# Layer 1 of a four-layer image kernel: a ninth VectorE product in third-slot jobs, and B rows spread in mid-unit in first-slot jobs

## The chip, the cores and the metric

The kernel runs on one core of a Trainium2 chip. The metric is the device time of that core in microseconds (us). Five engines work side by side, each with its own queue of instructions that it takes in order: TensorE (PE; its weight loads are listed as PEld), VectorE (DVE), ScalarE (ACT), GpSimd (POOL) and SyncE (SP, which here issues nearly all DMAs). They wait for one another through semaphores.

## The reference

The input is 8 images of 192 channels and 56 x 56 points, in float32. Four layers follow one another, each of the form x = x + f(group_norm(x)): layer 0 is an involution, layers 1 to 3 are Mamba blocks. The change concerns layer 1 alone. Its core is this recurrence (shortened):

```python
xn = layer_norm(x)                       # 192 channels, as three slices of 64
xs = stack of the three slices           # each goes through the same block
xi, z = split(xs @ in_proj_W.T)          # 512 inner channels each
xc = silu(causal_conv4(xi) + conv_b)
dbl = xc @ x_proj_W.T
dt = softplus(dbl[:4] @ dt_proj_W.T + dt_proj_b)
B, C = dbl[4:20], dbl[20:36]             # 16 states
h = h * exp(dt * A) + (dt * xc) * B      # for each point, channel and state
y = sum over states of h * C + xc * D
y = (y * silu(z)) @ out_proj_W.T
```

After it come a skip connection, a second layer norm over the three slices, and a projection to 192 channels. The points of an image form one sequence of 3136 steps, and h runs along it.

## The kernel before

**Tiling.** A chunk is 8 rows of an image, 448 points; there are 7 chunks to an image and 56 in all. In layer 1 each chunk makes three *jobs*, one for each slice of 64 channels; the number of the slice (0, 1, 2) is the job's *slot*, `jobs[i][0]`. So first-slot, second-slot and third-slot jobs follow in turn, 168 in all. A job has 512 inner channels in 4 groups of 128 (`nd == 4`), and each group is scanned in 4 *units* (`q`), so a job has 16 units, numbered `m` = 0 to 15, and layer 1 has 2688, numbered `k`. A unit holds 32 channels times 4 states on 128 partitions, and 4 runs of 448 points in the free dimension.

**What a unit needs.** (1) ScalarE writes exp(dt * A) into PSUM in two halves (`decays`, L761). (2) The product (dt * xc) * B goes into the buffer `uhg`. Either GpSimd makes it, from a B row that a DMA has spread over the partitions (`inputs_by_pool`, L782), or VectorE makes it, from a B row that a TensorE matmul has spread into a PSUM bank (`spread_b`, L749, then `inputs_by_vector`, L789). That bank, `banks.b`, has one buffer: the next spread must wait until the product that reads the present one is done. (3) VectorE scans the two halves in place (`scan`, L793). (4) ScalarE saves the last column for the next chunk (`keep`, L797). (5) GpSimd multiplies in place by the C row (`readout`, L802). (6) TensorE sums over the states into `y` (`reduce`, L811; the first unit of a group begins with L808). (7) One group later VectorE multiplies `y` into the gate (`gated`, L827), which frees the only `y` bank.

**Who makes which product.** `pool_units(i)` (L720 to L724) lists the units of a job whose product GpSimd makes: 1, 3, 7, 9, 11, 13 and 15 in every job, and besides unit 5 in first-slot jobs and in the last job, unit 6 in the others. So GpSimd and VectorE make eight each.

**Order.** The loop at L882 writes the order out by hand. In unit k every engine gets, in this order: the reduce of unit k-3; half 0 of scan k; the decays of unit k+1, half 0; GpSimd's product for unit k+2, if it is GpSimd's; the readout of unit k-2; VectorE's product for unit k+1, if it is VectorE's; the second planned place; half 1 of scan k; `keep`; the decays of k+1, half 1. In a job's unit 3 the product of unit 5, if VectorE's, is made early, right after scan 3 (L934).

Where the spread stands is the second thing of the change. In layers 2 and 3 (`nd == 3`) `spread_b(k + 2)` is called in mid-unit, ahead of the second planned place. In layer 1 (`nd == 4`) `spread_next_b(k + 1)` is called at the unit's end, behind the second planned place and ahead of half 1 of the scan. It spreads the next row that a VectorE product will want, as soon as the product before it has been put into VectorE's queue.

**The plan.** Each unit has two places in which steps of the *next* job are run: its convolution (L1069), the Silu block of ScalarE with its two table loads (L616, L597, L589; unit 3), the x-projection (L621), the delta projections (L632, L633, L655, moved out by L637 and L660), the Softplus block (L663, L589; unit 7 while a first-slot job runs, unit 9 otherwise), L667 and L670 behind it, and the gates (L1087, moved out by L694). The closing layer norm and projection of a chunk run during the first-slot job of the next one; the opening layer norm of the next chunk runs during the second-slot job. `nothing` (L817) adds matmuls with zeros where TensorE has little to do.

## Time and profile before

| | |
|---|---|
| median of 3 runs | 24,679.64 us (24,675.72 to 24,681.13) |
| the profiled execution | 24,712.5 us, span 24,710.4 us, mean granted TensorE clock 0.837 |
| busy over the span | POOL 94%, DVE 92%, PE 83%, ACT 69% |
| layer 1, from its first scan to layer 2's | 1,620.8 to 16,879.6 us |
| one chunk of it (window 13,790.6 to 14,060.3 us), its three jobs | 95.9 + 89.6 + 84.2 us |
| GpSimd busy in that chunk | 269.0 of 269.7 us |
| VectorE busy in that chunk | 252.3 of 269.7 us |
| one GpSimd product, one readout (layer 1, mean) | 3,992 ns, 3,675 ns |
| one VectorE product, one half scan (layer 1, mean) | 1,996 ns, 2,009 ns |
| one spread, full clock | 0.36 us |

A busy share is a mean over the span; what a change in layer 1 is worth shows in a chunk of layer 1. An engine's idle time is put down to what ended it. Durations overlap a little at their ends, so the step from one scan to the next counts for more than the sum of the means: a half scan takes 1.92 us from start to start, a VectorE product 1.93, a GpSimd product 3.95, a readout 3.64.

### The profile page before, as it was taken

To read this page: it belongs to the slowest core of one execution; us is meant where nothing else is said; L and a number is where in the kernel's file an instruction comes from. 1 tells how busy PE (TensorE), PEld (TensorE's weight loads), DVE (VectorE), ACT (ScalarE), POOL (GpSimd) and SP (SyncE) were. 2 spreads that over 40 slices of the span, in tenths; PEclk is the share of its full clock that TensorE was granted. 3 is DMA by queue.
4 is the path that set the end of the run, shared out by engine and by line. 5 is a ranking of instruction groups with operands and counts; after the bars stand their busy time and mean duration, and the time that the engine had idled before them with its cause. 6 is when DMAs were issued, how large, how long until landed. Compare 5 with 4: busy or idle time off the path is not lost.

```text
span 24710.4 us, 238275 instructions
## 1 busy us (share of the span) xinstructions
PE 20615.4 (83%) x74330; PEld 6482.2 (26%) x74330; DVE 22834.6 (92%) x15771; ACT 17044.6 (69%) x32578; POOL 23167.0 (94%) x6886
## 2 busy tenths in 40 slices
PE   8988888888888888888888888887888888888888
PEld 2222222222222222222222222222333322333332
DVE  8989999999999999999999999997999998999999
ACT  2247777777777777777777777776777776777776
POOL 5679999999999999999999999997999987999999
PEclk9987777778777887887887788788899888999998
DMA  4433333333333333333333333333444443444443
GB/s 109 109 107 128 128 127 128 126 124 129 127 126 128 128 128 123 129 128 126 128 128 126 126 129 128 127 127 114 135 135 140 140 137 122 140 144 141 140 140 128
DMA packets 1209092, 3171.54 MB, mean 128 GB/s; under 512 B 166444, under 2 KB 470596, under 8 KB 1207688
## 3 DMA queue, kind: packets, MB, share of 16 engines
q1 hardware_dynamic: 1205016, 3155.25, 38.8%
q8 instruction: 583, 9.55, 0.2%
q14 instruction: 693, 5.68, 0.1%
q10 hardware_dynamic: 2800, 1.06, 0.0%
HBM read 2438.45 MB, written 555.55 MB: 121 GB/s over the span
## 4 chain that ended last, share of the span: by engine, by line
DVE 28%; PE 22%; POOL 19%; issue 12%; ACT 12%; DMA 5%; SPq 1%; DVEq 0%; POOLq 0%; ACTq 0%
DVE uhg L793 19%; POOL uhg L802 12%; POOL uhg L782 6%; DVE uhg L789 6%; ACT da L761 5%; DMA rows<-bc 4%; PE y L811 4%; PE mm L655 3%; PE mm L1152 2%; PE mm L429 1%; PE mm L632 1%; PE y L808 1%; PE y_inv L467 1%; DVE prod L441 1%; PE mm L1099 1%
## 5 line engine op out<-in xcount | busy, mean ns | idle before, releaser
L793 DVE TENSOR_TENSOR_SCAN uhg<-da,uhg 128x898 f32<-128x898 f32 x8064 | 15893.3, 2010 | 729.2 <-ACT da L761 716.0
L802 POOL TENSOR_TENSOR uhg<-uhg,rows 128x1792 f32<-128x1792 f32 x4032 | 14734.2, 3676 | 185.3 <-ACT carry L797 181.6
L761 ACT ACTIVATE da<-rep,k 128x448 f32<-128x448 f32 x16128 | 10261.3, 636 | 1762.8 <-DVE uhg L793 1437.1
L782 POOL TENSOR_TENSOR uhg<-rep,rows 128x1792 f32<-128x1792 f32 x1906 | 7610.6, 3993 | 738.3 <-DMA rows<-bc 500.3
L811 PE MATMUL y<-uhg,k 128*32 128x448 f32 x32256 | 4647.7, 654 | 696.6 <-POOL uhg L802 692.4
L789 DVE TENSOR_TENSOR uhg<-rep,b 128x1792 f32<-128x1792 f32 x2126 | 4246.9, 1998 | 296.8 <-PE b L749 252.4
L797 ACT COPY carry<-uhg 128x4 f32<-128x4 f32 x4032 | 786.1, 195 | 3420.0 <-DVE uhg L793 3351.9
L817 PE MATMUL y<-w_d,k 128*128 128x448 f32 (+1 forms) x5276 | 2380.7, 553 | 0.0
L808 PE MATMUL y<-xc,w_d 128*128 128x448 f32 x2016 | 1526.7, 853 | 1004.1 <-DVE zs L827 1003.8
L811 PEld LDWEIGHTS y<-uhg,k 128*32 128x32 f32 x32256 | 680.2, 116 | 3492.2 <-issue 1917.4
L1125 PE MATMUL mm<-v,w_in 96*128 96x448 f32 x2688 | 1335.2, 625 | 188.3 <-ACT zs L696 85.0
L817 PEld LDWEIGHTS y<-w_d,k 128*128 128x128 f32 x5276 | 988.2, 203 | 1567.0 <-issue 1541.5
L1087 PE MATMUL mm<-xs,k 64*128 64x448 f32 x1344 | 893.1, 769 | 509.6 <-ACT zs L694 479.2
L655 PE MATMUL mm<-dbl,w_dt 36*128 36x448 f32 (+1 forms) x2016 | 1290.4, 756 | 1.9 <-ACT k L637 0.5
L749 PE MATMUL b<-k,k 96*128 96x448 bf16 x2126 | 809.0, 381 | 460.3 <-DVE uhg L789 459.8
L1069 PE MATMUL mm<-xs,k 128*128 128x448 f32 x2688 | 1119.8, 558 | 18.6 <-DMA xs<-xg 8.1
L667 PE MATMUL mm<-xc,k 128*128 128x448 f32 x2016 | 1032.6, 630 | 94.4 <-DVE dt L670 94.4
L1152 PE MATMUL mm<-xin,w_conv 128*128 128x448 f32 x2688 | 1077.9, 543 | 0.9 <-ACT xin L696 0.9
L441 DVE TENSOR_TENSOR prod<-mm,shifted 128x448 f32<-128x448 f32 x1680 | 929.9, 613 | 152.8 <-PE mm L429 77.1
L632 PE MATMUL mm<-dbl,k 16*16 16x448 f32 x1120 | 696.7, 711 | 441.7 <-ACT dbl L625 434.1
L808 PEld LDWEIGHTS y<-xc,w_d 128*128 128x128 f32 x2016 | 467.7, 269 | 1836.0 <-DVE zs L827 1348.9
L670 DVE TENSOR_TENSOR dt<-dt,mm 128x448 f32<-128x448 f32 x1008 | 594.0, 611 | 329.3 <-ACT dt L663 134.4
(138 smaller groups left out, 19659.1 us busy)
## 6 DMA issues: line engine op xcount, KB each, us to landing
rep<-ops SPq DMA_DIRECT2D x4032, 448.0 KB, 5.8
ops<-dt SPq DMA_DIRECT2D x1008, 448.0 KB, 3.1
rows<-bc SPq DMA_DIRECT2D x1960, 224.0 KB, 6.2
shifted<-xpad SPq DMA_DIRECT2D x672, 179.0 KB, 4.4
xg<-stream SPq DMA_DIRECT2D x168, 336.0 KB, 3.8
xr<-stream SPq DMA_DIRECT2D x168, 336.0 KB, 4.9
stream<-xr SPq DMA_DIRECT2D x112, 336.0 KB, 7.3
xs<-xg SPq DMA_DIRECT2D x224, 112.0 KB, 2.3
```

Of the source, the lines that this page charges most:

```text
L441: nc.vector.tensor_mul(prod.rearrange("p (h w) -> p h w", w=WW), fbs[item][: 128 if kind == "four" else CP, :T].rearrange("p (h w) -> p h ...
L655: nc.tensor.matmul(u.dps[j][:, :T], lhsT=w.dtw[:, j * 128 : (j + 1) * 128], rhs=u.dbl[:nk, :], start=True, stop=True)
L761: nc.scalar.activation(t[:, 64 + 449 * r : 512 + 449 * r], reps[k // NQ][:, 2 * h + r, 0, :], AF.Exp, scale=w.neg_a[:, j * NR + 2 * h + r, ...
L782: nc.gpsimd.tensor_mul(uhg[k][:, :, 1:], reps[k // NQ][:, :, 1, :], b)
L789: nc.vector.tensor_mul(uhg[k][:, :, 1:], reps[k // NQ][:, :, 1, :], b)
L793: nc.vector.tensor_tensor_scan(v, banks.da[h][:, 63:961], v, 0.0, ALU.mult, ALU.add)
L802: nc.gpsimd.tensor_mul(v, v, us[i].rows[1, q].unsqueeze(1).to_broadcast([128, NR, T]))
L808: nc.tensor.matmul(ys[k // NQ][:, :T], lhsT=w.dd[:, j, :], rhs=us[i].xc[:, j, :], start=True, stop=False)
L811: nc.tensor.matmul(y[32 * r : 32 * r + 32, :T], lhsT=fold, rhs=uhg[k][:, r, 1:], start=False, stop=(q == NQ - 1))
L817: nc.tensor.matmul(ys[k // NQ][:, : nd * 112], lhsT=zeros, rhs=w.dd.rearrange("p j e -> p (j e)")[:, : nd * 112], start=False, stop=False,)
L1125: nc.tensor.matmul(pm[:, :T], lhsT=w.inw[:, k, m * 128 : (m + 1) * 128], rhs=ck.v[:, k, :], start=(k == 0), stop=(k == NCT - 1),)
L1152: nc.tensor.matmul(pm[:, :T], lhsT=w.convd[:, j, k, :], rhs=ck.xin[:, j, k : k + T], start=(k == 0), stop=(k == 3))
```

## The change

In third-slot jobs unit 6 leaves GpSimd's list: GpSimd makes seven products there and VectorE nine (0, 2, 4, 5, 6, 8, 10, 12, 14). The last job of the layer stays as it was. The row for it is spread by TensorE, one spread more in each of 55 jobs. In first-slot jobs the rows are spread as in layers 2 and 3: `spread_b(k + 2)` in mid-unit k, where before the same row was spread at the end of unit k-1. In second-slot and third-slot jobs `spread_next_b` stays at the unit's end.

```diff
         def pool_units(i):
 
             if nd == 4:
-                return {1, 3, 6 if jobs[i][0] and i + 1 < len(jobs) else 5, 7, 9, 11, 13, 15}
+                fixed = {1, 3, 7, 9, 11, 13, 15}
+                if jobs[i][0] == 0 or i + 1 == len(jobs):
+                    return fixed | {5}
+                return fixed | ({6} if jobs[i][0] == 1 else set())
             return {1, 3, 7, 9, 11} | ({6} if i + 1 == len(jobs) else set())
...
+            rows_between = nd == 3 or jobs[i][0] == 0
...
                 inputs_by_vector(k + 1)
-            if nd == 3 and k + 2 < n_units:
+            if rows_between and k + 2 < n_units:
                 spread_b(k + 2)
             bg.run(plan[2 * m + 1])
-            if nd == 4:
+            if not rows_between:
                 spread_next_b(k + 1)
```

## The prediction

> **What bounds the kernel now.** First the page, part 2 (busy tenths in 40 slices of 618 us; layer 1 fills slices 3 to 27):

> ```profile
> DVE  8989999999999999999999999997999998999999
> POOL 5679999999999999999999999997999987999999
> PEclk9987777778777887887887788788899888999998
> ```

> Both VectorE and GpSimd stand at 9 in layer 1, so shares don't tell which one binds. Next, one steady chunk by its three jobs (columns: window; its length; busy us and instructions of PE, PEld, DVE, ACT, POOL; granted clock; DMA share; GB/s):

> ```profile
> 13790.60:13886.50 95.90, 82.26 (x239) 23.10 (x241) 87.09 (x55) 66.54 (x126) 95.90 (x27) 0.73 0.36 121
> 13886.50:13976.10 89.60, 71.58 (x240) 21.28 (x235) 83.63 (x51) 67.10 (x129) 89.37 (x24) 0.80 0.35 119
> 13976.10:14060.30 84.20, 70.67 (x248) 20.64 (x248) 81.62 (x49) 62.24 (x120) 83.77 (x23) 0.87 0.41 143
> ```

> GpSimd works 269.0 of 269.7 us, VectorE 252.3. Then the waits in that chunk, first GpSimd's, then VectorE's (total, times, longest):

> ```profile
> POOL uhg L782 <- DMA rows<-bc: 0.4, 1, 0.4
> POOL uhg L802 <- ACT carry L797: 0.2, 1, 0.2
> ```

> ```profile
> DVE uhg L793 <- ACT da L761: 6.5, 7, 1.6
> DVE uhg L789 <- PE b L749: 4.4, 2, 3.8
> DVE zs L827 <- PE y L811: 2.5, 2, 1.4
> DVE dt L670 <- PE mm L667: 1.3, 2, 0.9
> ```

> GpSimd sets the pace: 48 readouts of 3.64 and 24 products of 3.95 us, start to start, are 269.5 us, the chunk. VectorE idles 17 us, but only part of that is GpSimd's doing, and this part is all that a lighter GpSimd can give back. Two numbers from the timeline (start of a readout less the end of the `keep` before it) say how close VectorE is: 9.5 us at the end of a third-slot job, where GpSimd is far behind, and 0.1 us at unit 4 of the second-slot job, where it has caught up and hangs on VectorE. So one change of pace of 0.1 us there makes VectorE the bound.

> **The change part by part**, in us per chunk, on the profiled execution (24,712.5, span 24,710.4; it ran 33 over the median).

> *The product leaves GpSimd:* 3.95 less in each of 55 third-slot jobs. GpSimd then needs 265.5.

> *It comes to VectorE:* +1.93, between the halves of scan 5; that job has 81.6 of 84.2 busy, so nothing there hides it. Behind it on VectorE stand scan 5 half 1 and scan 6; `keep` 5 and readout 5 wait for those. Readout 5 had 7.1 us to spare and keeps about 1.2.

> *Its spread* (one weight load, one matmul, 0.36) takes the place at the end of unit 4 that unit 8's row had, about 3.8 us before the product wants it; unit 8's row goes to the end of unit 5, still some 5 us early. In front of reduce 3 this is 0.4, against 1.93 that VectorE is later. Cost 0; were TensorE over 3.8 late, it would show on VectorE one for one. The B row for GpSimd (q = 2) is still loaded and nobody reads it: SP's queue and its DMAs do not change. Zero matmuls do not change either.

> *What GpSimd's relief gives back.* Third-slot job, unit 10:

> ```profile
> 14028.13 2.03 DVE L793 TENSOR_TENSOR_SCAN uhg<-da,uhg 128x898 f32<-128x898 f32 x1 [0.75 <-ACT da L761]
> 14029.09 0.96 PE L811 MATMUL y<-uhg,k 128*32 128x448 f32 x8 [2.09 <-POOL uhg L802]
> 14029.98 1.77 PE L667 MATMUL mm<-xc,k 128*128 128x448 f32 x4
> 14031.04 1.37 DVE L670 TENSOR_TENSOR dt<-dt,mm 128x448 f32<-128x448 f32 x2 [0.88 <-PE mm L667]
> ```

> The reduce waits for a late readout, L667 stands behind it, VectorE waits 0.88. With GpSimd 5.9 (3.95 + 1.93) nearer this goes: -0.88. In the first-slot job, units 6 and 7:

> ```profile
> 13825.64 0.55 PE L749 MATMUL b<-k,k 96*128 96x448 bf16 x1
> 13826.63 1.72 PE L811 MATMUL y<-uhg,k 128*32 128x448 f32 x8 [0.44 <-POOL uhg L802]
> 13828.28 3.35 PE L655 MATMUL mm<-dbl,w_dt 36*128 36x448 f32 x4
> 13828.42 0.62 DVE L827 TENSOR_TENSOR zs<-zs,y 128x448 f32<-128x448 f32 x1 [1.43 <-PE y L811]
> 13831.67 0.63 ACT L660 ACTIVATE dt<-mm,k 128x448 f32<-128x448 f32 x1 [0.86 <-PE mm L655]
> ```

> Readout 3 holds the reduce, this holds VectorE's gate and L655, and L655 holds ScalarE's Softplus block, after which VectorE waits 0.74 + 0.98 + 1.47. What remains without GpSimd shows in the chunk from 4,861.3 us: GpSimd enters it 1.6 us less far behind (7.8 against 9.4), the gate waits are gone, and its first-slot job takes 93.9 instead of 96.0. The waits on ScalarE's blocks stay even there (2.84 at unit 4, 3.19 at units 7 and 8, 0.94 at unit 13). So -2.1 and no more. The changed kernel enters the job about 4.5 behind, past that point.

> *First-slot jobs, the spread in mid-unit.* Unit 8's row (0.55 at half clock, above) goes from in front of reduce 3 to behind L655: the Softplus chain starts up to 0.55 earlier. Between 0 and -0.55 I take -0.5, since ScalarE waits for L655. Two products get their row late, if TensorE keeps its times: unit 6 (behind L621) by 0.86 on average, unit 8 (behind L655) by 1.16. For unit 8, 0, since scan 7's second half waits 0.74 and L670 0.98 anyway. For unit 6, between 0 and 0.86, I take 0: its spread leaves the end of unit 3 (0.4) and TensorE's 0.7 wait for GpSimd at unit 4 goes. The other rows have 2.1 to 6.9 to spare. TensorE no longer waits for VectorE with a spread in unit 9 (3.2); only the layer norm stands behind, for which VectorE does not wait: 0.

> *The seam to the second-slot job.* Unit 2's row was spread at the end of the first-slot job's unit 15. That call is gone, and `spread_next_b` comes next at the end of unit 0, behind eight passes of L1069:

> ```profile
> 13888.87 0.36 PE L749 MATMUL b<-k,k 96*128 96x448 bf16 x1
> 13890.05 3.27 PE L1069 MATMUL mm<-xs,k 128*128 128x448 f32 x8
> 13892.29 2.00 DVE L789 TENSOR_TENSOR uhg<-rep,b 128x1792 f32<-128x1792 f32 x1
> ```

> L1069 ends at 13,893.3, the product started at 13,892.3: +1.1 (over all jobs 1.24 on average, 0.5 to 3.2 in eight of ten). It lies on VectorE just ahead of the place where GpSimd has 0.1 to spare, so nothing covers it.

> Sum for an ordinary chunk: -2.1 - 0.5 + 1.1 + 1.93 - 0.88 = -0.45, and GpSimd idles 3.5. In the 8 chunks that open an image GpSimd already catches up in the first-slot job (104.0 long, readouts 0.1 us behind at its end), so of its 2.6 only 0.5 counts, and the third-slot wait is 1.16: -0.5 + 1.1 + 1.93 - 1.16 = +1.4. Together 47 x -0.45 + 8 x 1.4 = -10. So 24,702 for an execution like the profiled one, **24,670** against the median.

> *TensorE's clock* is the least certain term. In the second-slot job VectorE waits for unit 5's row 3.85 in the steady chunk, where half clock was granted for 6.8 us from unit 3 on, 2.14 in the chunk at 4,861 (3.4 us of half clock) and 0.55 in chunks without it; the mean is 2.95. I leave it as it is. [...]

> **The rivals.**

> *GpSimd stays the bound.* All of its 3.95 comes through: 55 x 3.95 = -217, 24,463. For it: its waits, 0.6 us a chunk. Against: VectorE would have to give up 5.9 us of waits plus the seam's 1.1, and I find 3.5 that are GpSimd's. Half of it needs luck with the clock (3.85 becoming 2.14: 47 x -1.7 = -80, 24,590).

> *VectorE is the bound already.* Nothing is recovered, and the late rows are paid on VectorE: 1.93 + 1.1 + 0.86 = 3.9 a chunk, +214, 24,894. For it: the 0.1 us at unit 4 of the second-slot job. Against: the waits on L811 and L667 above. It decides once less than 2.1 of the 3.5 us comes back.

> *The change does nothing* is ruled out: 55 instructions leave GpSimd's queue and join VectorE's.

> **How the numbers follow.** A measurement here tells about 0.2% (49 us) from no change. My forecast has 0.46; its own range is 24,590 to 24,750 (1.5 us a chunk for the clock): 0.34 within 0.2%, 0.07 below, 0.05 above. The faster rival, in part or in full, has 0.27 (0.01 of it within 0.2%); the slower one 0.27 (0.03 within). So faster 0.33, same 0.38, slower 0.29. From 24,520 to 24,830 leaves out about 0.09 at each end.

> **What would show it.** Right: GpSimd idle 3 to 4 us a chunk, waiting for `carry`; the gate waits of first-slot jobs gone and those jobs near 93.5; a new wait of about 1.1 for `b` in second-slot unit 1; third-slot jobs near 85.2. Wrong, faster: GpSimd still without idle time, chunks near 266. Wrong, slower: chunks over 271, with waits of VectorE for `b` in first-slot units 5 and 7, or the Softplus waits grown under half clock.

## The result, and the profile after

The changed kernel takes 24,794.57 us (median; 24,772.89 to 24,824.98) against 24,681.13 us for the kernel before on the same chip: a ratio of 1.0043, 95% interval 1.0031 to 1.0055. It is slower by 0.43%, 113 us. The forecast was 24,670, so the sign was missed, though the time lies inside the stated range of 24,520 to 24,830.

The page of the changed kernel (its profiled execution took 24,794.57 us, span 24,792.7), parts 2, 4 and 5; lines from 724 to 902 have moved down by 3, later ones by 4:

```profile
DVE  8989999999999999999999999997999998999999
POOL 6679999999999999999999999997999987999999
PEclk9987777777777777777777777778899888999999
...
DVE 35%; PE 27%; ACT 14%; issue 13%; POOL 5%; DMA 5%; SPq 1%; DVEq 0%; POOLq 0%; ACTq 0%
...
L805 POOL TENSOR_TENSOR uhg<-uhg,rows 128x1792 f32<-128x1792 f32 x4032 | 14737.2, 3674 | 479.0 <-ACT carry L800 468.8
...
L670 DVE TENSOR_TENSOR dt<-dt,mm 128x448 f32<-128x448 f32 x1008 | 599.5, 612 | 444.3 <-ACT carry L800 162.5
```

The shares of part 2 hardly move. What moved is who waits for whom. GpSimd's share of the chain that ended last is 5% (it was 19%), and its readouts now wait 479 us, 469 of them for ScalarE's carries. The change did take the pace away from GpSimd. The chain runs over VectorE, TensorE and ScalarE instead. `L670` stands out: a small VectorE operation with 444 us of idle time in front of it.

Layer 1, from its first scan to layer 2's, went from 15,258.8 to 15,375.1 us: the whole loss is there (between these two executions the rest came out 34 us shorter). By jobs (from scan to scan; means of 56 first-slot, 56 second-slot and 55 third-slot jobs, without the last one, which runs into layer 2): first-slot jobs 96.29 to 93.99, second-slot 89.03 to 90.54, third-slot 85.04 to 88.01; -2.30 + 1.51 + 2.97 = +2.2 us a chunk. Three chunks that follow one another, windows by job, as in the fence of the prediction (window; length; busy us and instructions of PE, PEld, DVE, ACT, POOL; granted clock; DMA share; GB/s):

```profile
13584.24:13676.91 92.67, 81.16 (x237) 23.02 (x239) 86.74 (x55) 66.63 (x126) 92.25 (x26) 0.73 0.38 124
13676.91:13765.77 88.86, 69.86 (x240) 20.91 (x236) 83.74 (x51) 67.10 (x129) 87.05 (x24) 0.83 0.35 121
13765.77:13853.79 88.02, 77.09 (x250) 22.07 (x250) 83.62 (x51) 62.53 (x120) 85.81 (x24) 0.80 0.39 136
13853.79:13946.45 92.66, 81.05 (x237) 22.93 (x239) 86.76 (x55) 66.62 (x126) 92.29 (x26) 0.73 0.38 126
13946.45:14038.35 91.90, 73.38 (x240) 21.77 (x236) 83.96 (x52) 67.09 (x129) 87.48 (x24) 0.80 0.35 117
14038.35:14126.61 88.26, 76.02 (x249) 22.19 (x250) 83.62 (x51) 62.47 (x120) 85.51 (x23) 0.82 0.40 137
14126.61:14220.96 94.35, 79.11 (x237) 22.89 (x239) 86.96 (x55) 66.64 (x126) 92.41 (x26) 0.76 0.38 122
14220.96:14312.10 91.14, 72.05 (x240) 21.53 (x236) 83.74 (x52) 67.11 (x129) 86.67 (x24) 0.80 0.34 116
14312.10:14400.01 87.91, 76.92 (x250) 22.11 (x250) 83.62 (x50) 62.46 (x120) 86.14 (x24) 0.80 0.41 140
```

Chunks take 269.6, 272.8 and 273.4 us, in this order, again and again; chunks that open an image are longer. First-slot jobs fell to 92.7, below the forecast of 93.5, in two of the three. Third-slot jobs take 88, not 85.2, in all. Two things in these windows led to the experiments. VectorE's waits over the three chunks:

```profile
DVE uhg L792 <- PE b L752: 14.0, 11, 3.3
DVE dt L670 <- ACT carry L800: 9.6, 3, 3.4
...
DVE dt L670 <- ACT da L764: 3.2, 1, 3.2
```

There are four waits of 3.2 to 3.4 us at `L670`, one in each third-slot job and one in the second-slot job of 91.9. The names behind the arrow are not the cause: the timeline of unit 9 of a third-slot job shows who was late.

```profile
14087.62 4.31 PE L820 MATMUL y<-w_d,k 128*128 128x448 f32 x6
...
14088.83 1.70 ACT L663 ACTIVATE dt<-dt 128x1792 f32<-128x1792 f32 x1
...
14092.75 1.77 PE L667 MATMUL mm<-xc,k 128*128 128x448 f32 x4
...
14093.86 1.32 DVE L670 TENSOR_TENSOR dt<-dt,mm 128x448 f32<-128x448 f32 x2 [3.39 <-ACT carry L800]
```

`L670` multiplies Softplus's output by `L667`'s. Softplus was done at 14,090.5. `L667` starts only at 14,092.8, behind six passes of zeros (`L820`) that take 4.31 us (the granted clock was 0.50 up to 14,091.25, and 1.00 after), and a reduce of 0.96. The zeros belong to TensorE's unit 8 in the order of the loop; it runs them while VectorE is in unit 9.

The second thing: 269.6 + 272.8 + 273.4 = 815.8 us, and in both traces the granted clock changes in steps of 3.413 us: it is 0.50 (half clock) or 1.00 (full clock), and 1,649 of the 1,650 stretches of one clock before, 1,691 of the 1,692 after, have a length within 0.06 us of a whole multiple. 239 x 3.4133 = 815.8. A chunk of the kernel before, 269.65, is 79 of these steps, and the three chunks after are 79.67 on average.

### The profile page after: what moved, and what is told of

Its sections match the earlier page's. It is cut to its first block, busy times and chain, and to the rows that moved or that the text cites. A ratio compares the mean times of both kernels' runs of the same rounds, so it can differ in the third digit from the quotient of the medians.

```text
span 24792.7 us, 238268 instructions
## 1 busy us (share of the span) xinstructions
PE 20817.1 (84%) x74385; PEld 6545.3 (26%) x74385; DVE 22915.6 (92%) x15826; ACT 17053.6 (69%) x32578; POOL 22956.7 (93%) x6831
## 2 busy tenths in 40 slices
DVE  8989999999999999999999999997999998999999
## 4 chain that ended last, share of the span: by engine, by line
DVE 35%; PE 27%; ACT 14%; issue 13%; POOL 5%; DMA 5%; SPq 1%; DVEq 0%; POOLq 0%; ACTq 0%
DVE uhg L796 24%; DVE uhg L792 7%; ACT da L764 6%; PE y L814 5%; PE mm L655 4%; POOL uhg L805 3%; DMA rows<-bc 3%; PE y L811 2%; PE mm L632 2%; PE y L820 2%; PE mm L1156 2%; POOL uhg L785 2%; PE mm L667 2%; ACT L589 1%; DMA rep<-ops 1%
## 5 line engine op out<-in xcount | busy, mean ns | idle before, releaser
L785 POOL TENSOR_TENSOR uhg<-rep,rows 128x1792 f32<-128x1792 f32 x1851 | 7382.7, 3989 | 767.6 <-DMA rows<-bc 535.0
L814 PE MATMUL y<-uhg,k 128*32 128x448 f32 x32256 | 4690.6, 657 | 266.0 <-POOL uhg L805 263.9
L792 DVE TENSOR_TENSOR uhg<-rep,b 128x1792 f32<-128x1792 f32 x2181 | 4357.2, 1998 | 358.5 <-PE b L752 312.5
L811 PE MATMUL y<-xc,w_d 128*128 128x448 f32 x2016 | 1506.9, 843 | 1227.8 <-DVE zs L830 1227.7
L820 PE MATMUL y<-w_d,k 128*128 128x448 f32 (+1 forms) x5276 | 2449.1, 569 | 0.0
L814 PEld LDWEIGHTS y<-uhg,k 128*32 128x32 f32 x32256 | 691.6, 116 | 3119.7 <-issue 2128.5
L820 PEld LDWEIGHTS y<-w_d,k 128*128 128x128 f32 x5276 | 1018.7, 209 | 1640.7 <-issue 1614.5
L655 PE MATMUL mm<-dbl,w_dt 36*128 36x448 f32 (+1 forms) x2016 | 1411.2, 818 | 12.6 <-ACT k L637 12.6
L632 PE MATMUL mm<-dbl,k 16*16 16x448 f32 x1120 | 710.1, 723 | 515.2 <-ACT dbl L625 500.9
L667 PE MATMUL mm<-xc,k 128*128 128x448 f32 x2016 | 1019.2, 623 | 97.5 <-DVE dt L670 97.5
L670 DVE TENSOR_TENSOR dt<-dt,mm 128x448 f32<-128x448 f32 x1008 | 599.5, 612 | 444.3 <-ACT carry L800 162.5
L811 PEld LDWEIGHTS y<-xc,w_d 128*128 128x128 f32 x2016 | 460.2, 264 | 1992.3 <-DVE zs L830 1504.3
```

Of the source, the lines that this page charges most:

```text
L655: nc.tensor.matmul(u.dps[j][:, :T], lhsT=w.dtw[:, j * 128 : (j + 1) * 128], rhs=u.dbl[:nk, :], start=True, stop=True)
L667: nc.tensor.matmul(u.xps[j][:, :T], lhsT=ident, rhs=u.xc[:, j, :], start=True, stop=True)
L785: nc.gpsimd.tensor_mul(uhg[k][:, :, 1:], reps[k // NQ][:, :, 1, :], b)
L792: nc.vector.tensor_mul(uhg[k][:, :, 1:], reps[k // NQ][:, :, 1, :], b)
L811: nc.tensor.matmul(ys[k // NQ][:, :T], lhsT=w.dd[:, j, :], rhs=us[i].xc[:, j, :], start=True, stop=False)
L814: nc.tensor.matmul(y[32 * r : 32 * r + 32, :T], lhsT=fold, rhs=uhg[k][:, r, 1:], start=False, stop=(q == NQ - 1))
```

## The experiments

All times are medians. A ratio is to the kernel before, which ran alternately with it on the same chip: 24,685.70 us for the first four kernels, 24,679.04 for the next four, then 24,705.49, 24,695.03 and 24,688.73. "Steps" are chunk lengths from scan to scan in the trace, divided by 3.4133 us.

### Which part carries the loss

Theory V: VectorE's chain became the bound, and the loss sits in third-slot jobs. Rival R: it is the handing out of rows. First each part alone, then the changed kernel with one thing put back or taken away.

The product alone (first-slot jobs keep the order of before), and the rows alone (GpSimd keeps its product):

```diff
-            rows_between = nd == 3 or jobs[i][0] == 0
+            rows_between = nd == 3
```

```diff
             # on the kernel before
-            if nd == 3 and k + 2 < n_units:
+            if (nd == 3 or jobs[i][0] == 0) and k + 2 < n_units:
                 spread_b(k + 2)
...
-            if nd == 4:
+            if nd == 4 and jobs[i][0]:
                 spread_next_b(k + 1)
```

> The product move alone: third-slot jobs have VectorE make the ninth product, but in first-slot jobs the row of B goes out at the unit's end, as in the kernel before. Theory V (VectorE's chain has become the bound, and the loss sits in third-slot jobs, where the pause of TensorE ahead of Softplus leaves it at half clock into unit 9): third-slot jobs stay near 88.0 us, with VectorE's wait for L667 of about 3.2 us in unit 9, first-slot jobs come back to 93.5 to 96 and second-slot jobs to 89.0 to 89.5, for without the rows handed over ahead the second-slot unit 1 and 2 waits go; per chunk 270.5 to 273.2, that is +20 to +165 us against before. Rival R (the rows handed out in mid-unit carry the loss): third-slot jobs 85.2, chunk 268 or less, 0 to -95 us against before.

> The rows alone: GpSimd keeps its eight products in third-slot jobs as before, and in first-slot jobs rows of B are handed out in mid-unit. Theory V: the seam costs about 1.04 us in second-slot unit 1, first-slot jobs gain 0 to 0.5, third-slot jobs stay at 84.1 to 85.0; 0 to +55 us against before. Rival R: the rows carry the loss, +80 to +115 us against before, with third-slot jobs at 87 to 88 though GpSimd still makes the product.

The seam put back, and the zero matmuls of unit 8 taken away:

```diff
-            if not rows_between:
+            if not rows_between or nd == 4 and m == per_job - 1:
                 spread_next_b(k + 1)
```

```diff
             more = 3 - math.ceil(load_of(plan[2 * m] + plan[2 * m + 1]))
+            if nd == 4 and jobs[i][0] and m == 8:
+                more = 0
```

> The changed kernel, and in addition the row for second-slot unit 2 may go out at the end of the last unit of the first-slot job, as before. Theory V: the wait for b of 1.04 us in second-slot unit 1 goes and nothing takes its place: -57 us against the changed kernel, so about +55 against before. A rival (VectorE would meet the next wait, that for L670 or the carries, a microsecond later anyway): 0 to -15 us against the changed kernel.

> The changed kernel without the zero matmuls of unit 8 in second-slot and third-slot jobs (they add nothing to the sum; they run ahead of L667's matmuls in TensorE's queue). Theory V: in third-slot jobs L667 starts up to 4.5 us earlier and VectorE's wait of 3.2 us in unit 9 goes: third-slot jobs 85.0 to 85.5, about -160 us against the changed kernel, -45 against before. Rival S (the wait in unit 9 comes from the carries or rows, as its label says, and not from TensorE's queue): no change, within 20 us of the changed kernel. A third outcome: without the zeros half clock lasts longer and half of the gain or all of it goes back, 0 to -80.

| kernel | time | ratio, 95% interval | jobs, mean | steps |
|---|---|---|---|---|
| changed | 24,794.57 | 1.0043 (1.0031 to 1.0055) | 94.0 / 90.5 / 88.0 | 79, 80, 80 |
| product alone | 24,738.42 | 1.0020 (1.0010 to 1.0029) | 94.5 / 88.9 / 88.1 | 79, 80 |
| rows alone | 24,815.42 | 1.0050 (1.0035 to 1.0065) | 95.7 / 91.4 / 85.7 | 79 to 81.2 |
| changed, seam put back | 24,674.37 | 0.9992 (0.9983 to 1.0001) | 93.5 / 89.0 / 87.7 | 79 |
| changed, no zeros in unit 8 | 24,688.75 | 0.9999 (0.9990 to 1.0008) | 94.9 / 90.3 / 85.3 | 79 |

Third-slot jobs lengthen to 88 with the product, and to 85.7 with the rows: that half of V holds, and R falls for these jobs. But the seam costs 120 us, twice what V gave it and what its wait of 1.04 us in second-slot unit 1 explains; rows alone lose 130, where V had 0 to 55 and R 80 to 115; and without the zeros the third-slot job falls by the 2.7 us that V expected, but the total by 106 and not by 160, since first-slot jobs take up 0.9 of it. The parts don't add up by their microseconds. Whole steps do come out: two quite different repairs both end at 79.

### Does time go in steps?

Theory G: the chunk settles on whole steps of the 3.41 us grid, so a small delay is free and a larger one costs a step. Rival L: delays add up along VectorE. One pair repeats part of a VectorE product in second-slot jobs, on the changed kernel and on the version with the seam put back:

```diff
+            if nd == 4 and jobs[i][0] == 1 and m == 3:
+                b = brow[k + 1][:, :T].unsqueeze(1).to_broadcast([128, 1, T])
+                nc.vector.tensor_mul(uhg[k + 1][:, :1, 1:], reps[(k + 1) // NQ][:, :1, 1, :], b)
```

> The changed kernel with 0.5 us more work for VectorE: in second-slot jobs it makes a quarter of the product of unit 4 twice, with the same values. Theory G: in a third of the chunks the second-slot job reaches unit 5 just ahead of a clock change and pays a wait of 3.6 us in unit 9; half a microsecond later it no longer does, so the kernel becomes faster by 0 to 125 us though it does more. Rival L (delays add up along VectorE): 55 x 0.5 = +27 us.

> The same 0.5 us of VectorE work added to the version with the restored seam, where the second-slot jobs pay no wait in unit 9. Theory G: chunks stay at 79 steps of the grid, since the wait in unit 9 of the third-slot job, which ends on the clock's return, takes the delay up: 0 +- 10 us. Rival L: +27 us.

They came to 24,777.22 (1.0035, 1.0022 to 1.0048) and 24,652.23 (0.9988, 0.9978 to 0.9998), with nearly the same chunk patterns as without the delay. The repair that G expected of the first did not come, and neither run speaks for G or against it: the place was badly chosen, for just behind it VectorE waits for the row of unit 5 (with the seam put back 3.8 us), and this wait shrank (to 3.1). The second pair puts the delay where no wait stands behind it for 8 units (`n` is 1 or 4):

```diff
             # on the version with the seam put back
+            if nd == 4 and jobs[i][0] == 2 and m == 11:
+                b = brow[k + 1][:, :T].unsqueeze(1).to_broadcast([128, n, T])
+                nc.vector.tensor_mul(uhg[k + 1][:, :n, 1:], reps[(k + 1) // NQ][:, :n, 1, :], b)
```

> The version with the restored seam, and VectorE makes a quarter of the product of unit 12 in third-slot jobs twice (0.6 us; no wait stands between this place and unit 4 of the next job, so nothing there can hide it). Theory G: ordinary chunks stay at 79 steps (269.65 us), the delay comes out of a wait that ends on a clock change: 0 +- 10 us. Rival L: 55 x 0.6 = +33 us.

> The same with the whole product of unit 12 made twice (1.95 us). Theory G: either still 79 steps, 0 +- 15 us, or up to a pattern of 79.33, 79.5 or 80 steps, +62, +94 or +188 us, and nothing between. Rival L: 55 x 1.95 = +107 us, 79.57 steps per chunk without a pattern.

A chunk with the 0.6 us, and one with the 1.95 us (windows by job):

```profile
13801.68:13894.64 92.96, 80.77 (x237) 23.06 (x239) 86.77 (x55) 66.63 (x126) 91.75 (x25) 0.75 0.38 125
13894.64:13982.71 88.07, 69.48 (x240) 20.76 (x236) 83.63 (x52) 67.12 (x129) 87.00 (x24) 0.83 0.36 122
13982.71:14071.34 88.63, 77.15 (x250) 22.06 (x250) 84.24 (x52) 62.49 (x120) 86.58 (x25) 0.80 0.39 136
sum 269.66, PE 227.40 PEld 65.88 DVE 254.63 ACT 196.24 POOL 265.32; mean PE 75.80 PEld 21.96 DVE 84.88 ACT 65.41 POOL 88.44
```

```profile
sum 273.06, PE 227.74 PEld 66.62 DVE 256.22 ACT 196.10 POOL 265.45; mean PE 75.91 PEld 22.21 DVE 85.41 ACT 65.37 POOL 88.48
```

With 0.6 us the chunk stays at 269.66, 79 steps: the third-slot job is 0.8 longer, first-slot and second-slot jobs give it back. With 1.95 us it is 273.06, 80 steps, in every ordinary chunk of the settled part. The totals are 24,685.22 (0.9996, 0.9986 to 1.0005) and 24,897.26 (1.0080, 1.0065 to 1.0095). So 0.6 us was free in ordinary chunks, though not everywhere: chunks that open an image went from 80 to 81 steps. And 1.95 us cost 3.4 to 6.9 a chunk, some 220 us more than the version it was added to (by the ratios), where adding up gives 107. For the 0.6 us the totals alone can't tell G's 0 from L's 33; the chunk lengths can. G holds, L falls.

### What keeps TensorE at half clock

In nine kernels that have the zeros, I put together for each second-slot job, that of the first chunk left out, how long the half clock lasted that begins in unit 5, and VectorE's idle time ahead of `L670` in units 9 and 10. In 399 jobs it lasted 13.7 us and the wait was 0 to 0.54; in 87 it lasted 20.5 us and the wait was 3.59 to 3.86. There is nothing between. Is it the pause of 4 us ahead of `L632` that brings this on? The next two kernels fill it with zero matmuls (`n` is 8 or 4) on the version with the seam put back.

```diff
             nothing(k - 3, more > 1)
+            if nd == 4 and jobs[i][0] and m == 4:
+                nothing(k - 3, n)
```

> The version with the restored seam, and eight more zero matmuls at the end of unit 4 of second-slot and third-slot jobs, so that TensorE works through most of the 4 us in which it otherwise waits for L625 in unit 5. Theory G (the wait in unit 9 comes from the half clock that this pause brings on; whether it comes and how long it lasts depends on where the pause falls on the 3.41 us grid of clock changes): no half clock, or a shorter one, in units 5 to 9, VectorE's waits for L670 in unit 9 fall from about 2.9 us to under 0.5 in third-slot jobs, these take 84.9 to 85.3 us; about -2.5 us per chunk, -100 to -190 us against the version with the restored seam (24,674), so 24,480 to 24,570. Rival N (the half clock follows from the thin matmuls L632 and L655 and not from the pause): no shorter half clock, and no gain; up to +30 us if the zeros delay L632.

> The version with the restored seam and four zero matmuls (eight passes, 3.0 us) at the end of unit 4 in second-slot and third-slot jobs, so that TensorE's pause in unit 5 shrinks from 4.0 us to 1.0 and L632 is not held up. If the pause brings on the half clock: VectorE's wait in unit 9 of third-slot jobs falls from 2.9 us to under 0.5, third-slot jobs take 85.3, and the time changes by 0 to -190 us. If the thin matmuls behind it (L632, the reduces of 32 rows) bring it on: half clock still sets in, 3 to 7 us later, the wait stays above 2 us, and the time stays within 30 us of 24,674.

Eight were too many (two passes each, 6 us, so `L632` came 2 us late): 24,797.97 (1.0044, 1.0027 to 1.0061). Four left `L632` nearly in place and still lost: 24,873.22 (1.0072, 1.0056 to 1.0089), 80 steps, waits of mostly 3.1 us (second-slot jobs) and 3.6 us (third-slot jobs) in unit 9. Half clock began later in the job (by 4.1 us in second-slot, 1.4 in third-slot jobs) and then stayed for 17.1 and 20.5 us, though TensorE was busy. So filling the pause put off the start of half clock and did not do away with it.

The end shows when the trace is cut at the places where the clock can be seen to change, into windows of 3.413 us. Below, TensorE's passes on tile `y` (all use 128 rows: `L811`, `L814`, `L820`) in single clock windows of units 7 to 9; after the busy columns (PE, PEld, DVE, ACT) stands the granted clock. Third-slot job of the kernel before:

```profile
14014.67:14018.09 3.42, 3.42 (x10) 0.66 (x10) 0.00 (x0) 0.00 (x0) 0.50 0.94 315
14018.09:14021.50 3.41, 1.49 (x14) 0.52 (x11) 0.00 (x0) 0.00 (x0) 1.00 0.29 116
```

Changed kernel, third-slot job:

```profile
14077.60:14081.01 3.41, 2.25 (x6) 0.71 (x10) 0.00 (x0) 0.00 (x0) 0.50 0.93 315
14081.01:14084.42 3.41, 1.26 (x8) 0.00 (x0) 0.00 (x0) 0.00 (x0) 0.50 0.57 217
14084.42:14087.84 3.42, 1.87 (x9) 0.42 (x10) 0.00 (x0) 0.00 (x0) 0.50 0.02 5
14087.84:14091.25 3.41, 3.41 (x5) 1.63 (x6) 0.00 (x0) 0.00 (x0) 0.50 0.00 0
14091.25:14094.66 3.41, 1.87 (x11) 0.54 (x10) 0.00 (x0) 0.00 (x0) 1.00 0.00 0
```

Changed kernel, the second-slot jobs of 88.9 and of 91.9 us:

```profile
13719.20:13722.61 3.41, 2.64 (x10) 0.20 (x8) 0.00 (x0) 0.00 (x0) 0.50 0.68 264
13722.61:13726.02 3.41, 1.86 (x11) 0.76 (x12) 0.00 (x0) 0.00 (x0) 1.00 0.02 7
```

```profile
13988.85:13992.26 3.41, 2.58 (x10) 0.20 (x8) 0.00 (x0) 0.00 (x0) 0.50 0.74 274
13992.26:13995.68 3.42, 0.55 (x4) 0.20 (x8) 0.00 (x0) 0.00 (x0) 0.50 0.00 0
```

A window with 3.42 us of such passes is followed by full clock, and so is one with 2.64; one with 2.58 is not. TensorE was fully busy in both of the last two, the rest being `L655` with 36 rows. Over the 17 kernels other than the three tests below, half clock that begins in units 5 to 7 of second-slot or third-slot jobs ended 1,835 times: 1,818 times after a window with at least 2.6 us of 128-row passes. Of the 6,980 windows that did not end it, 24 had as much, none over 2.63, though TensorE was busy all through 4,911 of them. Of the windows with 2.56 to 2.6, 90 did not end it and one did. In the traces of before and after alone nothing overlaps: the 224 windows that ended it had at least 2.62 us, the other 865 at most 2.61. The 17 returns with less are all from one kernel (the last table's "before, no zeros, row early"): 16 had 2.1 to 2.3 us of such passes, and besides 0.56 us of a spread, with 96 rows; this stays unexplained. In units 7 and 8 there is one stretch of such passes, the start of a reduce (`L811`, 1.8 us, and the first `L814`, 1.7 us, at half clock): 3.5 us, which a grid line may cut so that neither window has 2.6 (2.25 and 1.26 in the third-slot job above). There half clock lasted until the zeros of unit 8, further on, filled a window (3.41), and these are what `L667` stands behind.

That is a reading of traces. The next three kernels test it by *adding* work: one more zero matmul behind that reduce makes the stretch 5 us long, so that wherever the grid falls some window has at least 2.5. It is added to the changed kernel, to the version with the seam put back, and to the fastest one (below).

```diff
             if k >= 3:
                 reduce(k - 3)
+            if nd == 4 and jobs[i][0] and m == 7:
+                nothing(k - 3, 1)
```

> The changed kernel, and one zero matmul more (two passes over 128 rows, 1.5 us at half clock) right behind the reduce in unit 7 of second-slot and third-slot jobs. Theory W (half clock ends after the first 3.41 us window in which passes with 128 rows take at least 2.6 us; thin passes of 16, 36 or 96 rows do not count): the stretch of 128-row passes in units 7 and 8 grows from 3.5 us to about 5.0, so wherever the grid falls some window holds nearly 2.6 us or more of it, full clock is back in unit 8, VectorE's waits of 3.2 to 3.6 us for L670 in unit 9 fall under 0.6 in most second-slot and third-slot jobs, third-slot jobs take 85.0 to 85.8, and the time goes down by 0 to 190 us (79 or 78.67 steps) although TensorE does more. Rival (half clock ends for some other reason, and TensorE is late anyway): waits as before or up to 1.5 us longer, 0 to +190 us.

> The same zero matmul in the version with the restored seam. Theory W: the wait of 2.9 us in unit 9 of third-slot jobs goes, third-slot jobs take 85.0 to 85.8; 78 or 78.5 steps per chunk, or still 79 if the time comes back in the first-slot job: -190 to 0 us against 24,674. Rival: no shorter half clock, 0 to +190 us.

> The same zero matmul in the fastest version so far (24,522), where the waits in unit 9 are gone already. Theory W: nothing left to win there, 78 steps stay, -20 to +20 us; 77 or 77.5 steps if the earlier clock saves a microsecond elsewhere. If the 1.5 us of TensorE work costs time, up to +190 us.

Changed kernel with the extra zeros, third-slot job, tile `y` in single clock windows:

```profile
14041.04:14044.45 3.41, 0.54 (x1) 0.50 (x2) 0.00 (x0) 0.00 (x0) 0.50 0.51 146
14044.45:14047.87 3.42, 3.42 (x11) 0.71 (x10) 0.00 (x0) 0.00 (x0) 0.50 0.93 331
14047.87:14051.28 3.41, 1.49 (x10) 0.16 (x8) 0.00 (x0) 0.00 (x0) 1.00 0.15 62
```

In 110 of the 111 jobs with a half clock from units 5 to 7 on, the window that ended it now held 3.41 us of these passes (2.84 in the other). Waits for `L670` of more than 2.5 us in units 9 and 10, of 55 second-slot and 55 third-slot jobs: 5 and 12 before, 19 and 54 after the change, 0 and 0 here. Third-slot jobs went from 88.0 to 85.7. More work on TensorE made VectorE's wait go away, as Theory W had it. The total went down by much less: 24,760.32 (1.0030, 1.0019 to 1.0041), 79 and 80 steps in turn; second-slot jobs went from 90.5 to 91.9, as VectorE's waits for rows in their units 1 and 3 grew from 3.5 to 4.9. With the seam put back it stayed at 79 steps and 24,679.36 (0.9998, 0.9988 to 1.0007). The 2.2 us of the third-slot job came back in the other two, where VectorE still waits 4.0 us for the row of unit 5 in second-slot unit 3. The 2.2 us are less than a step, and the chunk stayed at its 269.65 us.

### What the change is worth without these waits

The remaining kernels take the wait for the row of unit 5 away as well, and separate the terms of the prediction.

Seam put back and no zeros in unit 8; and with, besides, the row of unit 5 handed out ahead of `L1101` and `L1103`:

```diff
+            if nd == 4 and jobs[i][0] and m == 3:
+                spread_next_b(k + 1)
             bg.run(plan[2 * m + 1])
```

> The version with the restored seam, and without the zero matmuls of unit 8 in second-slot and third-slot jobs. Added up from the jobs of the two single edits: 93.0 + 89.0 + 85.3 = 267.3 us per chunk, 2.3 less than either, about -125 us against 24,674. Theory G (chunk times sit on whole steps of the 3.41 us grid, or fractions where a pattern of chunks repeats): 78, 78.33 or 78.5 steps, 266.2 to 268.0, -190 to -90 us; if the chunk falls back to 79 steps (269.7), no gain at all.

> The version with the restored seam and without the zero matmuls of unit 8, and the row of B for unit 5 of second-slot and third-slot jobs goes out in unit 3 ahead of the ten passes of L1101 and L1103, not behind them. VectorE's wait for this row in second-slot unit 3 (3.5 us) goes; the row's matmul itself waits for VectorE's product of unit 4 and holds TensorE up by about 1 us. Theory G (chunks take whole steps of the 3.41 us grid of clock changes, or fractions of it where a pattern of chunks repeats): 78 steps instead of 79, -3.4 us per chunk, -190 us against 24,647, so about 24,460; if the saving is not enough for a step, none of it shows. Rival L (times add up): -2.5 to -3.5 us per chunk, -140 to -190 us. The two part only if the chunk comes to rest between two steps.

The same two edits on the kernel before:

> The kernel before with the two edits of the fastest version (no zero matmuls in unit 8, the row for unit 5 handed out in unit 3 ahead of L1101 and L1103, both in second-slot and third-slot jobs), but with none of the change. If the change is worth something once the waits for TensorE in half clock are gone, this stays behind the fastest version's 24,522: 79 steps per chunk, about 24,650 to 24,690. If the change is worth nothing, it reaches 78 steps too, about 24,500 to 24,520.

GpSimd's relief alone, and VectorE's product alone, both on the kernel before:

```diff
-            if k >= 2:
+            if k >= 2 and not (nd == 4 and jobs[i][0] == 2 and m == 8):
                 readout(k - 2)
```

```diff
+            if nd == 4 and jobs[i][0] == 2 and m == 4 and i + 1 < len(jobs):
+                b = brow[k + 1][:, :T].unsqueeze(1).to_broadcast([128, NR, T])
+                nc.vector.tensor_mul(uhg[k + 1][:, :, 1:], reps[(k + 1) // NQ][:, :, 1, :], b)
```

> The kernel before, and in third-slot jobs GpSimd doesn't multiply unit 6 by its row of C (the readout, 3.64 us; the sum for y of that unit is then a different one). This takes about as much from GpSimd as the product does, gives VectorE nothing more to do, and moves no row. The prediction's relief term says: first-slot jobs fall by the waits that ended on GpSimd, from 96 to 93 to 93.5 us, nothing else moves, -2.5 to -3.3 us per chunk, -140 to -180 us. Theory G: 79 steps stay (0 +- 15 us, the 2.5 us come back as waits on the half clock in the later jobs) or the chunk drops to 78 (-188) or to 78.33 or 78.5 where a pattern repeats. Rival V0 (VectorE was the bound and GpSimd's load gave no time away): first-slot jobs stay at 96, no change.

> The kernel before, and VectorE makes the product of unit 5 in third-slot jobs twice (1.95 us more for VectorE; GpSimd and the rows as before). The prediction's sum: +1.93 per chunk where VectorE sets the pace of the third-slot job, less the 0.9 us of its wait in unit 10: about +1.0 per chunk, +57 us, with GpSimd catching up meanwhile, so that first-slot jobs fall by as much as GpSimd gains. Theory G: 79 steps (0 +- 15), or a step up, 79.33 to 80 (+62 to +188 us).

| kernel | time | ratio, 95% interval | jobs, mean | steps |
|---|---|---|---|---|
| seam put back, no zeros | 24,647.24 | 0.9987 (0.9978 to 0.9997) | 94.8 / 89.3 / 85.8 | 79 |
| and the row early | 24,521.61 | 0.9924 (0.9910 to 0.9939) | 94.4 / 87.0 / 85.7 | 78 |
| and the extra zeros in unit 7 | 24,506.90 | 0.9928 (0.9911 to 0.9944) | 94.5 / 87.2 / 85.4 | 78 |
| before, no zeros, row early | 24,660.28 | 0.9983 (0.9973 to 0.9992) | 95.8 / 88.1 / 85.9 | 78.1 to 79.5 |
| before, GpSimd relieved | 24,540.96 | 0.9934 (0.9920 to 0.9949) | 95.1 / 89.4 / 83.3 | 78 |
| before, one product twice | 24,701.29 | 1.0009 (0.9998 to 1.0020) | 95.4 / 89.6 / 85.9 | 79, for six chunks 80 |

A chunk of the version with the row early, and VectorE's waits in it:

```profile
13617.42:13710.99 93.57, 82.45 (x240) 23.75 (x242) 86.91 (x55) 66.64 (x126) 93.49 (x26) 0.72 0.38 124
13710.99:13798.10 87.11, 69.84 (x234) 20.30 (x230) 83.55 (x51) 66.86 (x129) 86.02 (x24) 0.79 0.36 122
13798.10:13883.58 85.48, 69.93 (x240) 20.25 (x241) 83.41 (x50) 62.25 (x120) 85.48 (x24) 0.82 0.41 141
sum 266.16, PE 222.22 PEld 64.30 DVE 253.87 ACT 195.75 POOL 264.99; mean PE 74.07 PEld 21.43 DVE 84.62 ACT 65.25 POOL 88.33
```

```profile
DVE uhg L792 <- PE b L752: 0.9, 2, 0.5
DVE dt L670 <- PE mm L667: 0.6, 1, 0.6
...
DVE dt L670 <- ACT dt L663: 0.5, 2, 0.3
```

Seam and zeros alone stayed at 79 steps: of the 2.0 us that third-slot jobs lost, first-slot jobs took back 1.4. With the row early, the waits for rows and at `L670`, 4.3 and 3.6 us a chunk with the seam put back alone, are down to 0.9 and 1.1, the chunk is at 78 steps, and GpSimd, with 265.0 of 266.2 us, sets the pace again. This beats both kernels: 0.76% faster than before. By the ratios, the early row brought some 155 us, less than the 190 of a whole step in every chunk. The same two edits without the change give 0.17%: GpSimd's work of some 269 us a chunk is then the floor, and the chunks wander between 78.1 and 79.5 steps. So the change, with the seam put back, is worth some 0.6% once TensorE is not late. Relief of GpSimd alone brings 154 us, but not where it was expected: first-slot jobs lose 1.2 us of 96.3 and not 2.5 to 3.3, and third-slot jobs, which were to stay, lose 1.7; the product's 1.95 us on VectorE alone costs nothing that can be told from zero, since VectorE has that much to spare as long as GpSimd sets the pace.

## Why the prediction was wrong

**The product leaves GpSimd; GpSimd idles 3.5 us.** Right. It idles 6.6 us a chunk after (19.8 over the three chunks shown). VectorE's waits for GpSimd's work do give time back: the kernel before with GpSimd relieved gains 2.8 us a chunk, in first-slot and third-slot jobs. The 3.5 were put for a chunk of 269.3 us; chunks came to 271.9. GpSimd's waits over the three chunks:

```profile
POOL uhg L805 <- ACT carry L800: 17.9, 13, 4.5
POOL uhg L785 <- DMA rows<-bc: 1.9, 1, 1.9
```

**First-slot jobs, -2.1 and -0.5, near 93.5.** Right: 92.7 in two of three chunks, 94.4 in the third, -2.30 on average. The gate waits went (1.04 to 0.17 us in unit 6). The wait for decays in unit 4, which the prediction read as 2.84 in the chunk at 4,861, is now 2.87 on average (1.78 before).

**The seam, +1.1.** Its own wait was sized right, 1.04 us on average, but this is 0.6 to 0.7 in most chunks, where TensorE is back at full clock early in unit 0, and 3.26 in 8 of the 55, where it goes through unit 0 and into the eight passes at half clock (in the chunk that begins at 14,126.61 the granted clock is 0.50 up to 14,227.8). And it has a second effect that the prediction did not have. It moves the second-slot job against the grid, so that in 19 of 55 chunks (5 before, 2 with the seam put back) the window in unit 8 holds 2.42 to 2.60 us of 128-row passes, half clock goes on through it, and units 9 and 10 pay 3.6. The seam is not the only thing that can do this: with the product alone, and rows handed out as before, there are 24 such chunks. Putting the seam back gave 120 us, not 57.

**Third-slot jobs, +1.93 - 0.88, 85.2.** This is the step that failed: "With GpSimd 5.9 nearer this goes: -0.88". GpSimd's relief by itself does take this wait away: in the kernel before with GpSimd relieved, VectorE's waits in a third-slot job have no `L670` left:

```profile
DVE uhg L793 <- ACT da L761: 1.0, 2, 0.7
DVE uhg L789 <- PE b L749: 0.6, 1, 0.6
```

In the changed kernel the wait in unit 10 did shrink, from 1.02 to 0.34 us. But `L667` stands behind the zeros of unit 8 as well, which the prediction put at nothing because they do not change. TensorE's chain from `L632` on now falls at a place of the grid where half clock lasts 20.5 to 23.9 us instead of, mostly, 10.2 to 13.7, and unit 9 waits 3.2 (0.8 before). The job takes 88.0. That VectorE is 1.93 us later does not bring this on by itself: in the kernel before with the product made twice VectorE has just as much more to do there, half clock mostly lasts 17.1 us, and such a wait stands in 8 of 55 third-slot jobs (12 before, 54 after the change). Why the changed loop settles on just this place of the grid stays open.

**"TensorE's clock is the least certain term. I leave it as it is."** The range was widened for it, but at one place only, the row of unit 5 in the second-slot job, and this barely moved (2.95 to 2.51). The same clock in units 5 to 9 was not priced at all, though the kernel before has 12 third-slot jobs with such a wait.

**The sum.** Terms were added up in tenths of a microsecond. Chunks of most of these kernels came out at whole steps of 3.41 us: 79 before, 79, 80 and 80 after. That a sum of -0.45 could show as nothing or as a step, as the 0.6 us and the 1.95 us did, is what the prediction lacked.

**The rivals.** "VectorE is the bound already" had the right sign and was 100 us too high, by a wrong mechanism: it assumed that nothing is recovered, and in first-slot jobs 2.3 us were. "GpSimd stays the bound" (24,463 to 24,590) is close to what comes out when TensorE's lateness is taken away (24,507 to 24,522), so the gain that was looked for does exist.

## What to carry to other kernels

Where, as here, one engine's queue swings between half and full clock in every pass of the loop, first divide the period of the loop by the grid of the clock changes as the trace shows it (here 269.65 us by 3.413): if it is a whole number, or a simple fraction, savings below a step may not show and small delays may cost a whole one, as here 0.6 us was free and 1.95 us cost 3.4 or more a chunk. A wait that comes in two sizes with nothing between (here 0 to 0.54 and 3.59 to 3.86 us) was the sign of it, and the thing to repair was the place where the clock comes back late, not the sum of small costs. Look behind the name that a wait gives: `L670`'s said carry, while the late one was a matmul (`L667`) behind zeros at half clock.

## What the runs showed of the hardware

That the grid of the clock changes is what holds the chunks to whole steps rests on three things: the lengths (within a tenth of a step of a whole number in 34 of the 35 ordinary chunks after the first two images with the zeros taken away, in all 35 with 1.95 us added), the free 0.6 us and the 3.4 us for 1.95, and the waits of two sizes. No run holds the clock fixed, which would settle it. For the kernel before it can't be told, as GpSimd's own 269.5 us happen to lie next to 79 steps, 269.65.
